# Experts' silu taken straight from its matmul bank, and the last two of eight holographic parts of six chunks computed wholly among the experts

## The chip, the core and the metric

The kernel runs on one core of a Trainium2 chip. The metric is the time of one execution in microseconds, as the device measures it; the median of some runs is compared. The engines are PE (matmuls), DVE (vectors), ACT (activations), POOL (vectors, without access to the matmul banks) and SP, which here issues DMAs.

## The reference, cut

Sixteen sequences of 256 tokens of width 128 go through two layers, each with a modulated layernorm before its attention part and its feed-forward part. The parts that the change touches are the first layer's mixture of experts and the second layer's attention, which is holographic (running sums of rotated values).

```
gu   = einsum('th,ehf->tef', x, gate_up_proj) + gate_up_bias      # 16 experts
gate = minimum(gu[..., ::2], 7.0);  up = clip(gu[..., 1::2], -7.0, 7.0)
glu  = gate * sigmoid(gate * 1.702)
out  = einsum('te,teh->th', scores, einsum('tei,eih->teh', (up + 1) * glu, down_proj) + down_bias)

k = exp(1j * 10 * (x @ Wk));  v = x @ Wv                          # 16 heads of 64: 1024 channels
out_pos   = real(cumsum(v * rotors) * conj(rotors)) / sqrt(t)
out_assoc = real(cumsum(v * conj(shifted k)) * k) / sqrt(t)
out = (out_pos * gate_0 + out_assoc * gate_1) @ Wo
```

The feed-forward part of the second layer that follows (`r * (square(relu(k)) @ W_v)`, called the mixing here) is not changed, only placed differently.

## The kernel before

The tokens lie in eight chunks of two sequences, 512 tokens each. Three stages follow one another. In each, every engine's instructions run in the order in which the program issues them, so an instruction that waits holds up all behind it on its engine.

**Attention** (to 301 us) covers all 16 sequences in 64 rounds; the change adds two operations on POOL there, at round 40.

**Experts** (301 to 687 us). One loop runs over n, 128 steps of chunk c and expert e (16 a chunk). In step n PE computes `pg` (gate, L808) and `pup` (up, L810) of expert n and `acc` (down, L833) of expert n-3. DVE forms `g` = min(pg + bias, limit) (L812); ACT forms `u` = pup + bias (L814) and the silu of g, back into the bank of pg (L817); POOL clips u (L818). One step later DVE multiplies, `u` = (u + 1) * pg (L824), and POOL weighs the product with the scores, `u` = u * wide (L825), which `acc` reads. Three banks serve pg, two pup, one acc.

Beside this, the same loop carries other work, each piece issued at a step of its own, all of it through one bank, `p_m`:

- at steps 3 and 4 of a chunk the last chunk's result is turned (`pmo`, L849) and added to the stream (DVE, L855), at steps 5 to 7 its means, squares and spread follow (ACT, POOL), and at step 7 the scores of the next chunk are transposed (`psc`, L339) and copied by ACT (`scT`), from which a DMA spreads them (`wide`);
- `parts_ahead` computes parts of the second layer's attention for six of the eight chunks. There are eight parts of 128 channels (j = 0 to 7) to a chunk. From step 8 of one chunk it normalizes the tokens of the chunk before (step 8), turns them (10), computes the values `pv` of part 7 (12) and its keys `pk` (13), and their phases: ACT rounds (`off`), DVE subtracts (`off`, L985, step 14), ACT takes |off|, and two Sin (steps 14 and 15). Then, in the next chunk, come pieces, one a step at 12 of the 16 steps: POOL binds a value row to a rotation (`bound_ahead`, L957), and at the step after DVE sums it along the tokens (L961), multiplies with gate and rotation (L965) and adds (L967). The pieces are four of part 7 by keys ("assoc"), four of part 7 by position ("pos"), and four of part 6 by position, whose values are computed at step 5. A DMA writes the two sums to memory (`there`).

**Holographic stage** (687 to 1052 us). One loop over steps, one for each part that is left: 7 for each of the first six chunks (`PARTS`), 8 for the last two. In a full step n POOL multiplies the sums of step n-1 with their phasors (L1456) and binds the values of step n+1 in two products (L1235); DVE runs two sums along the tokens (L1238), the phases of step n+2 (L1213) and one product (L1450); PE computes the keys and values of step n+3 (L1197, L1201) and adds the two products to `pout` (L1252, four matmuls). The seventh step of the first six chunks is a half one (`is_half`): part 6 by keys alone, since its position half was computed ahead. The sums computed ahead are fetched by DMA at a chunk's second step and added by one matmul each, at the fourth step and at the half step. `place` puts the mixing of earlier chunks into these steps, by their distance from the chunk's end; its tiles and the turned results (`pho`) share two banks, `p_x`.

Of the kernel before, what the change touches and what calls it, by code (L numbers as in the profile page):

```python
# [18 lines left out]
P = 128  # L19
# [16 lines left out]
ALPHA, LIMIT = 1.702, 7.0  # L36
GONE = -3.0e38
# [6 lines left out]
PARTS = [NJ - 1 if c < AHEAD else NJ for c in range(NCH)]  # L44
# [11 lines left out]
def tile_adaln_two_layers(ctx: ExitStack, tc: tile.TileContext, a: dict, out: bass.AP):  # L56
# [206 lines left out]
    with ExitStack() as moe_scope:  # L263
# [87 lines left out]
        with ExitStack() as scope:  # L351
# [374 lines left out]
            for n in range(len(rounds) + LAG + 1):  # L726
                if n < len(rounds):
                    if n in next_chunks:
                        start(project(next_chunks[n]), rank=0)
                    if n in (len(rounds) - NR, len(rounds) - NR + 1):  # L730
                        start(first_scores(n - (len(rounds) - NR)))
                    s = scores(n)
                    with_maxima(n, row_maxima(n, s))
                take_step("dve")
                if LAG <= n < len(rounds) + LAG:
                    es[n - LAG] = weights(n - LAG)
                if n >= LAG + 2 and rounds[n - LAG - 2][1] == NR - 1:
                    b = rounds[n - LAG - 2][0]
                    start(chunk_end(b // 2) if b % 2 else attn_end(b))
                if n > LAG:  # L740
                    values(n - LAG - 1, es.pop(n - LAG - 1))
                take_step("mid")
                take_step("end")
                take_step("take", True)
                if later_loads:
                    later_loads.pop(0)()
                if n == len(rounds) - 1:

                    for q in range(2):
                        widened(q)  # L750
                if n < LAG:

                    for place in ("mid", "end", "take"):
                        take_step(place)
                take_step("after", True)
                take_step("late")
                if n == 1:
                    filled(1, nc.gpsimd)
                    later_constants()
            take_step("take", True)  # L760
# [26 lines left out]
        with ExitStack() as scope:  # L787
# [16 lines left out]
            def gate_up(n, between=None):  # L804
# [6 lines left out]
                g = mp3.tile([P, N], F32, tag="g", name=f"g_{n}")  # L811
                nc.vector.tensor_scalar(g, pg, b_gu[:, 0, e : e + 1], LIMIT, ALU.add, ALU.min)  # L812
# [4 lines left out]
                nc.scalar.activation(pg, g, AF.Silu, scale=ALPHA)  # L817
                nc.gpsimd.tensor_scalar(u, u, LIMIT, -LIMIT, ALU.min, ALU.max)  # L818
                work[n] = pg, u

            def act(n):
                c, e = divmod(n, NE)
                pg, u = work.pop(n)
                nc.vector.scalar_tensor_tensor(u, u, 1.0, pg, ALU.add, ALU.mult)  # L824
                nc.gpsimd.tensor_tensor(u, u, wide[n // SOME][:, n % SOME, :], ALU.mult)  # L825
                work[n] = u
# [102 lines left out]
            def parts_ahead(c):  # L929
# [30 lines left out]
                def read(q, nm, k, s, i, probe):  # L960
# [11 lines left out]
                assoc = [(j, "assoc", k, s, 1, cs[:, s, k, 0:T], cs[:, s, k, 1:]) for k in range(2) for s in range(2)]  # L972
                pos_, pos_before = (
                    [(q, "pos", k, s, 0, rotor[:, q, s, :], rotor[:, q, s, :]) for k in range(2) for s in range(2)]
                    for q in (j, j - 1)
                )
                yield
                pk = p_m.tile([P, 2, T], F32, tag="m", name=f"pk0_{c}")
                nc.tensor.matmul(pk, w_k1[:, ts(j, P)], flat, start=True, stop=True)
                off, size = (  # L980
                    cross.tile([P, 2, T], F32, tag="hn4", name=f"{nm}_ahead_{c}") for nm in ("off", "size")
                )
                nc.scalar.activation(off, pk, AF.Copy, bias=ROUND)
                yield
                nc.vector.scalar_tensor_tensor(off, off, ROUND, pk, ALU.subtract, ALU.subtract)  # L985
                nc.scalar.activation(size, off, AF.Abs)
                nc.scalar.activation(cs[:, 1, :, 1:], off, AF.Sin, scale=-TWO_PI_IN)
                yield
                nc.scalar.activation(cs[:, 0, :, 1:], size, AF.Sin, bias=half_pi, scale=-TWO_PI_IN)
                yield  # L990

                pieces = assoc + pos_ + pos_before
                late_one = None
                for step in range(1, NE + 1):
# [6 lines left out]

                    if step not in (4, 7, 11, NE):
                        late_one = pieces.pop(0)
                        bind(*late_one[:4], late_one[5])
# [162 lines left out]
    with ExitStack() as scope:  # L1167
# [55 lines left out]
        def is_half(n):  # L1223

            return steps[n][0] < AHEAD and steps[n][1] == NJ - 2

# [3 lines left out]
        def binders(n):  # L1230
            w = work[n]
            v2 = w["v"].unsqueeze(1).to_broadcast(both)
            for nm, bind in (("pos", rot(n)), ("assoc", phasor[n % 3][:, :, :, 0:T]))[is_half(n) :]:
                w[nm] = hp.tile(both, F32, tag=f"bound_{nm}", name=f"bound_{nm}_{n}")
                nc.gpsimd.tensor_tensor(w[nm], v2, bind, ALU.mult)  # L1235

        def summed(n, nm, dst, half=slice(0, 2)):
            nc.vector.tensor_tensor_scan(  # L1238
                dst[:, half].rearrange("p s k t -> p (s k t)"),
                keep.rearrange("p (s k) t -> p s k t", k=2)[:, half].rearrange("p s k t -> p (s k t)"),  # L1240
                work[n][nm][:, half].rearrange("p s k t -> p (s k t)"),
# [176 lines left out]
        for n in range(last + 2):  # L1418
# [3 lines left out]
            place = {n - begin[m + 1]: m for m in (c - 2, c - 1) if 0 <= m < NCH - 1 and n <= last}  # L1422
# [5 lines left out]
            if j == 4 and AHEAD <= c + 1 < NCH:  # L1428
                into_tokens(c + 1, pt_tokens)
            if n <= last:  # L1430
                half = is_half(n)
                mem = p_mem.tile(both, F32, tag="mem", name=f"mem_{n}")
                if not half:
                    m_pos = hp.tile(both, F32, tag="m_pos", name=f"m_pos_{n}")
                m_assoc = hp.tile(both, F32, tag="sum_assoc", name=f"sum_assoc_{n}", bufs=3)
                work[n]["m"] = m_assoc
                if half:

                    summed(n, "assoc", mem, slice(0, 1))
                    summed(n, "assoc", m_assoc, slice(1, 2))  # L1440
                elif n:
                    summed(n, "assoc", m_assoc)
                if not half:
                    summed(n, "pos", mem)
                if n and n + 2 <= last:
                    phases(n + 2)
                if half:
                    nc.vector.tensor_tensor(m_assoc[:, 0], mem[:, 0], phasor[n % 3][:, 0, :, 1:], ALU.mult)
                else:
                    nc.vector.tensor_tensor(m_pos, mem, rot(n), ALU.mult)  # L1450
                if n == 0:
                    summed(n, "assoc", m_assoc)
            if 1 <= n <= last + 1:
                m = work.pop(n - 1)["m"]
                part = slice(1 if is_half(n - 1) else 0, 2)
                nc.gpsimd.tensor_tensor(m[:, part], m[:, part], phasor[(n - 1) % 3][:, part, :, 1:], ALU.mult)  # L1456
# [42 lines left out]
            if n < last:  # L1499
                if is_half(n):  # L1500
                    with_fetched(c, j, w_last[:, 0])
                else:
                    out_project(n, 0, w_pos, m_pos)
                if j == 1 and c < AHEAD:
                    fetched(c)
                if j == 3 and c < AHEAD:
                    with_fetched(c, NJ - 1, w_last[:, 1])
# [19 lines left out]
            if j == 1 and AHEAD <= c + 1 < NCH:  # L1527
                tokens(c + 1)
            if 2 in place:
                mix_means(place[2], hp, hp)  # L1530
            if j == 3 and AHEAD <= c + 1 < NCH:
# [127 lines left out]
```

## Time and profile before

| | |
|---|---|
| median of 3 runs | 1076.47 us (1075.56 to 1076.85) |
| the profiled execution: span from first to last instruction | 1073.6 us |
| the profiled execution: own time | not on the page; the median is 2.9 us above the span |
| busy: PE, DVE, ACT, POOL | 1020.8, 913.2, 705.0, 796.7 us |
| DMA moved | 53.15 MB |
| mean granted clock of PE | 0.994 |

Rows of a group name the line, the engine, the operation, what is written and read, the shapes and the count; then busy time and the mean of one in ns, and the idle time of the engine before them. A matmul of 512 columns appears as two records of 592 ns that start 430 ns apart, so that one is 0.86 us of PE; rows of one engine may overlap by some 50 ns.

### The profile page before, as it was taken

The page shows a single profiled execution, that of the slowest core. Times are in us where ns is not written, and L with a number is a line of the kernel's source. Part 1 is how long each engine was busy: PE and PEld are TensorE (multiplying, and loading weights), DVE is VectorE, ACT ScalarE, POOL GpSimd, SP SyncE. Part 2 cuts the span into 40 slices and gives each one's busy share as a digit, 9 for nine tenths or more (in the row PEclk, how much of TensorE's full clock was granted, in tenths as well). Part 3 has the DMA queues.
Part 4 walks back from the last instruction along what each step waited for, and adds up shares of the span by engine and source line. Part 5 has one row for each costly group of instructions (what it writes and reads, how often), then busy time and mean ns, then how long its engine had stood idle before and what let it go on. Part 6 is the DMA issues. An engine that isn't in the chain of part 4 may idle for free.

```text
span 1073.6 us, 16224 instructions
## 1 busy us (share of the span) xinstructions
PE 1020.8 (95%) x5333; PEld 518.4 (48%) x5333; DVE 913.2 (85%) x1413; ACT 705.0 (66%) x1515; POOL 796.7 (74%) x754
## 2 busy tenths in 40 slices
PE   7999999999999999999999999898999999999987
PEld 5566766676654444444434434333444444444334
DVE  6679878998756798988878778999999999999995
ACT  3776677667656677687766746355767767767662
POOL 3245334533557678888878788899999999999992
PEclk9999999999999999999999999999999999999999
DMA  4102100000052222323222223100000000000000
GB/s 118 42 11 71 51 5 3 2 4 2 4 179 96 82 99 79 118 91 107 100 98 89 89 89 108 59 10 10 14 7 30 15 15 30 1 11 5 5 10 20
DMA packets 35538, 53.15 MB, mean 50 GB/s; under 512 B 8416, under 2 KB 23296, under 8 KB 35456
## 3 DMA queue, kind: packets, MB, share of 16 engines
q1 hardware_dynamic: 34912, 51.87, 14.8%
q8 instruction: 42, 0.69, 0.2%
q14 instruction: 40, 0.33, 0.1%
q10 hardware_dynamic: 544, 0.26, 0.1%
HBM read 46.34 MB, written 5.51 MB: 48 GB/s over the span
## 4 chain that ended last, share of the span: by engine, by line
PE 64%; POOL 15%; DVE 10%; issue 5%; ACT 5%; DMA 1%; SPq 0%; DVEq 0%; POOLq 0%; ACTq 0%
PE pout L1252 9%; PE pg L808 7%; PE acc L833 7%; PE pup L810 7%; PE s L440 5%; PE st L474 5%; PE po L494 5%; POOL u L825 3%; POOL bound_assoc L1235 3%; POOL bound_pos L1235 3%; POOL sum_assoc L1456 2%; PE pk L1197 2%; PE pv L1201 2%; DVE sum_assoc L1238 2%; DVE mem L1238 2%
## 5 line engine op out<-in xcount | busy, mean ns | idle before, releaser
L482 ACT ACTIVATE exp<-st 128x512 f32<-128x512 f32 x256 | 132.2, 603 | 85.9 <-PE st L474 85.9
L452 DVE TENSOR_REDUCE maxima<-s 128x2 f32<-128x512 f32 x256 | 159.0, 685 | 25.7 <-PE s L440 25.3
L825 POOL TENSOR_TENSOR u<-u,wide 128x512 f32<-128x512 f32 x128 | 164.6, 1286 | 16.5 <-DVE u L824 7.4
L833 PE MATMUL acc<-u,w_dn 128*128 128x512 f32 x256 | 133.9, 605 | 6.1 <-POOL u L825 6.1
L1238 DVE TENSOR_TENSOR_SCAN sum_assoc<-keep,bound_assoc 128x1024 f32<-128x1024 bf16 (+1 forms) x58 | 126.0, 2173 | 9.9 <-POOL bound_assoc L1235 9.9
L808 PE MATMUL pg<-hT,w_gu 128*128 128x512 f32 x256 | 131.9, 597 | 0.8 <-DVE logits L674 0.4
L810 PE MATMUL pup<-hT,w_gu 128*128 128x512 f32 x256 | 130.7, 592 | 0.0
L814 ACT ACTIVATE u<-pup,b_gu 128x512 f32<-128x512 f32 x128 | 87.0, 679 | 63.7 <-PE pup L810 55.7
L1235 POOL TENSOR_TENSOR bound_assoc<-v,phasor 128x1024 f32<-128x1024 f32 x57 | 124.2, 2179 | 1.7 <-ACT phasor L1221 1.7
L818 POOL TENSOR_SCALAR u<-u 128x512 f32<-128x512 f32 x128 | 80.4, 628 | 59.6 <-ACT u L814 53.4
L812 DVE TENSOR_SCALAR g<-pg,b_gu 128x512 f32<-128x512 f32 x128 | 95.4, 746 | 32.7 <-PE pg L808 32.4
L1456 POOL TENSOR_TENSOR sum_assoc<-sum_assoc,phasor 128x1024 f32<-128x1024 f32 (+1 forms) x58 | 120.9, 2085 | 0.3 <-DVE sum_assoc L1238 0.3
L1238 DVE TENSOR_TENSOR_SCAN mem<-keep,bound_pos 128x1024 f32<-128x1024 bf16 x52 | 118.3, 2275 | 0.0
L1252 PE MATMUL pout<-m_pos,w_pos 128*128 128x512 f32 x204 | 98.4, 605 | 13.5 <-ACT oT L1277 10.7
L1235 POOL TENSOR_TENSOR bound_pos<-v,rotor 128x1024 f32<-128x1024 f32 x51 | 111.1, 2178 | 0.0
L1252 PE MATMUL pout<-sum_assoc,w_assoc 128*128 128x512 f32 x228 | 108.2, 597 | 1.5 <-POOL sum_assoc L1456 1.4
L817 ACT ACTIVATE pg<-g 128x512 f32<-128x512 f32 x128 | 76.3, 596 | 42.3 <-DVE g L812 41.9
L824 DVE SCALAR_TENSOR_TENSOR u<-u,pg 128x512 f32<-128x512 f32 x128 | 86.9, 679 | 11.8 <-POOL u L818 9.9
L474 PE MATMUL st<-qx,kx 32*128 32x256 f32 x1024 | 81.6, 387 | 1.2 <-DMA qx<-turned 1.1
L833 PEld LDWEIGHTS acc<-u,w_dn 128*128 128x128 f32 x256 | 46.7, 191 | 74.3 <-issue 42.9
L440 PE MATMUL s<-kx,qx 32*128 32x256 f32 x1024 | 78.0, 407 | 4.2 <-DVE kx L577 1.8
L1219 ACT ACTIVATE phasor<-off 128x512 f32<-128x512 f32 x56 | 35.1, 627 | 70.0 <-DVE off L1213 68.5
(301 smaller groups left out, 1912.2 us busy)
## 6 DMA issues: line engine op xcount, KB each, us to landing
wide<-scores SPq DMA_DIRECT2D x64, 512.0 KB
qx<-turned SPq DMA_DIRECT2D x256, 1.0 KB
there<-total SPq DMA_DIRECT2D x12, 256.0 KB
fetched<-there SPq DMA_DIRECT2D x12, 256.0 KB
w_gu<-in_gate_up_dram SPq DMA_DIRECT2D x8, 256.0 KB
out_dram<-x SPq DMA_DIRECT2D x16, 128.0 KB
x<-in_x_dram SPq DMA_DIRECT2D x14, 128.0 KB
w_dn<-in_down_dram SPq DMA_DIRECT2D x4, 256.0 KB
```

Of the source, the lines that this page charges most:

```text
L440: nc.tensor.matmul(s[g][:, i, :], qs[c][r][rows_, k, ts(i, P)], ks[c][rows_, r // NS, k, :], start=True, stop=True,)
L452: nc.vector.tensor_reduce(mx[:, :, g], s[g], AX.X, ALU.max, negate=True)
L474: nc.tensor.matmul(st[g][:, i, :], ks[c][rows_, r // NS, k, ts(i, P)], qs[c][r][rows_, k, :], start=True, stop=True,)
L482: nc.scalar.activation(e[:, g, :, :], st[g], AF.Exp, scale=QSCALE)
L808: nc.tensor.matmul(pg, w_gu[:, e, 0 : 2 * D : 2], h2, start=True, stop=True)
L810: nc.tensor.matmul(pu, w_gu[:, e, 1 : 2 * D : 2], h2, start=True, stop=True)
L825: nc.gpsimd.tensor_tensor(u, u, wide[n // SOME][:, n % SOME, :], ALU.mult)
L833: nc.tensor.matmul(accs[c], w_dn[:, e, :], work.pop(n), start=False, stop=(e == NE - 1))
L1235: nc.gpsimd.tensor_tensor(w[nm], v2, bind, ALU.mult)
L1238: nc.vector.tensor_tensor_scan(dst[:, half].rearrange("p s k t -> p (s k t)"), keep.rearrange("p (s k) t -> p s k t", k=2)[:, half].rearra ...
L1252: nc.tensor.matmul(pos[c], w[:, j, :], m[:, k, :, :].rearrange("p k t -> p (k t)"), start=(j == 0 and i == 0 and k == 0), stop=(c < NCH - ...
L1456: nc.gpsimd.tensor_tensor(m[:, part], m[:, part], phasor[(n - 1) % 3][:, part, :, 1:], ALU.mult)
```

## The change

It has two parts.

In the experts, `g` and its DVE instruction go. ACT takes the silu from the bank of pg with the bias in the activation, `silu(1.702 * pg + 1.702 * bias)`, ahead of `u`; the limit is taken after the silu, as the silu's value at the limit (`MOST`), in DVE's product. The +1 of `up + 1` goes into the bias and into POOL's bounds. Two operations on POOL scale and shift the biases once, in the attention stage.

In `parts_ahead`, part 6 is computed whole, with keys of its own: `pk` of part 6 at step 6 of the chunk, its `off` and |off| at step 7, its Sin at step 8. There are 16 pieces, one at every step. The holographic stage then has six full steps for each of the first six chunks and no half step; the fetched sums are added at the fourth and the fifth step, and the mixing spreads over up to three later chunks.

```diff
+MOST = ALPHA * LIMIT / (1.0 + math.exp(-ALPHA * LIMIT))
-PARTS = [NJ - 1 if c < AHEAD else NJ for c in range(NCH)]
+PARTS = [NJ - 2 if c < AHEAD else NJ for c in range(NCH)]
...
+                if n == 40:
+
+                    nc.gpsimd.tensor_scalar(b_gu[:, 0, :], b_gu[:, 0, :], ALPHA, None, ALU.mult)
+                    nc.gpsimd.tensor_scalar(b_gu[:, 1, :], b_gu[:, 1, :], 1.0, None, ALU.add)
...
-                g = mp3.tile([P, N], F32, tag="g", name=f"g_{n}")
-                nc.vector.tensor_scalar(g, pg, b_gu[:, 0, e : e + 1], LIMIT, ALU.add, ALU.min)
+                nc.scalar.activation(pg, pg, AF.Silu, bias=b_gu[:, 0, e : e + 1], scale=ALPHA)
                 u = mp3.tile([P, N], F32, tag="u", name=f"u_{n}", bufs=4)
                 nc.scalar.activation(u, pu, AF.Identity, bias=b_gu[:, 1, e : e + 1])
...
-                nc.scalar.activation(pg, g, AF.Silu, scale=ALPHA)
-                nc.gpsimd.tensor_scalar(u, u, LIMIT, -LIMIT, ALU.min, ALU.max)
+                nc.gpsimd.tensor_scalar(u, u, LIMIT + 1.0, 1.0 - LIMIT, ALU.min, ALU.max)
...
-                nc.vector.scalar_tensor_tensor(u, u, 1.0, pg, ALU.add, ALU.mult)
+                nc.vector.scalar_tensor_tensor(u, pg, MOST, u, ALU.min, ALU.mult)
...
+                def phasors(q):
+                    pk = p_m.tile([P, 2, T], F32, tag="m", name=f"pk0_{c}_{q}")
+                    nc.tensor.matmul(pk, w_k1[:, ts(q, P)], flat, start=True, stop=True)
...
+                    nc.scalar.activation(off, pk, AF.Copy, bias=ROUND)
+                    yield
+                    nc.vector.scalar_tensor_tensor(off, off, ROUND, pk, ALU.subtract, ALU.subtract)
+                    nc.scalar.activation(size, off, AF.Abs)
+                    yield
+                    nc.scalar.activation(cs[:, 1, :, 1:], off, AF.Sin, scale=-TWO_PI_IN)
+                    nc.scalar.activation(cs[:, 0, :, 1:], size, AF.Sin, bias=half_pi, scale=-TWO_PI_IN)
...
+                pieces = [*pieces_of(j), *pieces_of(j - 1)]
+                late_one, next_ones = None, None
+                for step in range(1, NE + 2):
                     yield
                     if late_one:
                         read(*late_one[:5], late_one[6])
                         late_one = None
                     if step == 5:
                         vs[j - 1] = values(j - 1)
-
-                    if step not in (4, 7, 11, NE):
+                    if step == 6:
+                        next_ones = phasors(j - 1)
+                    if next_ones:
+                        next_ones = next_ones if next(next_ones, 0) is None else None
+                    if pieces:
                         late_one = pieces.pop(0)
                         bind(*late_one[:4], late_one[5])
...
-            place = {n - begin[m + 1]: m for m in (c - 2, c - 1) if 0 <= m < NCH - 1 and n <= last}
+            place = {n - begin[m + 1]: m for m in (c - 3, c - 2, c - 1) if 0 <= m < NCH - 1 and n <= last}
...
-                if is_half(n):
-                    with_fetched(c, j, w_last[:, 0])
-                else:
-                    out_project(n, 0, w_pos, m_pos)
+                out_project(n, 0, w_pos, m_pos)
                 if j == 1 and c < AHEAD:
                     fetched(c)
-                if j == 3 and c < AHEAD:
-                    with_fetched(c, NJ - 1, w_last[:, 1])
+                if j in (3, 4) and c < AHEAD:
+                    with_fetched(c, NJ + 2 - j, w_last[:, 4 - j])
```

The rest of the diff takes `is_half` and its branches out, and counts the steps at which the last two chunks' tokens are prepared from a chunk's end.

## The prediction

> **What bounds the kernel now.** I read the page first, then the busy time by stretch, then each stage's groups and waits, and last the timeline around one step that the change fills. The kernel has three stages: attention (0 to 301 us), the experts (301 to 687 us) and the holographic stage (687 to 1052 us). The change leaves the first alone.
>
> ```profile
> PE 1020.8 (95%) x5333; PEld 518.4 (48%) x5333; DVE 913.2 (85%) x1413; ACT 705.0 (66%) x1515; POOL 796.7 (74%) x754
> core 0: us, PE busy (x) PEld busy (x) DVE busy (x) ACT busy (x) POOL busy (x), PEclk, DMA share, GB/s
> 488.10:534.50 46.40, 46.40 (x118) 20.91 (x117) 37.80 (x67) 36.33 (x87) 38.49 (x48) 1.00 0.29 103
> 783.90:827.20 43.30, 41.91 (x106) 18.86 (x106) 42.71 (x37) 30.72 (x67) 43.22 (x23) 1.00 0.06 19
> 827.20:870.60 43.40, 41.95 (x107) 18.97 (x107) 42.71 (x37) 30.94 (x67) 43.28 (x23) 1.00 0.06 19
> ```
>
> The first row is the whole kernel. The second gives the columns of the rest: 488.1 to 534.5 us is one chunk of the experts, the two others are one chunk each of the holographic stage. In the experts' chunk PE is busy for all 46.4 us and DVE, ACT and POOL have 8 to 10 us to spare. In a holographic chunk three engines are full at once: POOL 43.2, DVE 42.7, PE 41.9 of 43.3. So work taken out of the holographic stage is worth what it costs on the fullest of the three, and work put into the experts is worth what it costs PE, or makes PE wait. The clock is 1.00 in all of them.
>
> **What the holographic stage loses.** Six chunks have six full steps and one half step; the half step goes. These are its rows, all others are the full steps':
>
> ```profile
> L1235 POOL TENSOR_TENSOR bound_assoc<-v,phasor 128x1024 f32<-128x1024 f32 x57 | 124.2, 2179 | 1.7 <-ACT phasor L1221 1.7
> L1456 POOL TENSOR_TENSOR sum_assoc<-sum_assoc,phasor 128x512 f32<-128x512 f32 x6 | 7.6, 1267 | 0.0
> L1238 DVE TENSOR_TENSOR_SCAN mem<-keep,bound_assoc 128x512 f32<-128x512 bf16 x6 | 7.4, 1231 | 0.2
> L1238 DVE TENSOR_TENSOR_SCAN sum_assoc<-keep,bound_assoc 128x512 f32<-128x512 bf16 x6 | 7.2, 1204 | 0.0
> L1448 DVE TENSOR_TENSOR sum_assoc<-mem,phasor 128x512 f32<-128x512 f32 x6 | 4.2, 692 | 0.0
> L1213 DVE SCALAR_TENSOR_TENSOR off<-whole,pk 128x512 f32<-128x512 f32 x56 | 37.9, 676 | 0.0
> ```
>
> For each chunk POOL loses one bind (2.18 us, 2.13 from start to start) and a half product (1.27, 1.24 from start to start): 3.37 us. DVE loses 1.23 + 1.20 + 0.69 + 0.68 = 3.80. PE loses pk, pv and two pout; each is two records 0.43 us apart, so 4 x 0.86 = 3.44. The smallest counts, POOL's: 6 x 3.37 = 20.2 us. A chunk becomes 39.9 us. Nothing is late next by much, since the other two fall by more, but PE stays close: 41.9 - 3.4 = 38.5 busy, plus the one wait a chunk for oT (10.7 us over 7 times, 1.5 each), is 40.0. And the mixing that used seven steps is packed into six: in the changed kernel's order `pk2` falls in a chunk's second step and gets the bank of `pho`, which DVE gives back only at the end of its queue for that step. DVE runs ahead of PE there by up to a step, so I take no loss, and 1 us a chunk (6 in all) as the other end.
>
> **What the experts get.** PE gets one `pk` matmul more per chunk (the `pv` was there already): 6 x 0.86 = 5.1 us, on the path, since PE is full.
>
> DVE loses 128 g (0.746 us, 95.4 us in all) and gets 24 more pieces: 24 x (0.69 scan + 0.49 product) and 24 additions of 0.425, with 6 off of 0.68, 42.6 us. POOL gets 24 binds of 0.68, 16.4 us, and two 128x16 operations in the attention stage (a 128x4 one of the same kind takes 0.24), which nothing there waits for. ACT's silu takes its bias from a column now: 0.596 becomes about 0.69, because Sin with a bias column takes 0.712 and without one 0.614, 12 us in all; the other end is the 0.679 of `u`, which also reads PSUM. Six more phasors on ACT take 0.59 + 0.63 + 0.61 + 0.71 each, 15.3 us. All of this lies beside PE, which covers it: ACT has 10 us to spare in a chunk and needs 1.5 + 2.5. Without the cover it would cost 27 us.
>
> A rule speaks against putting more Sin between the silus: the Trainium skill, "ScalarE: Activation LUTs", section "What ACT_TABLE_LOAD costs", states about 2.66 us for each switch to another table set. Twelve more switches would by it be an estimated 32 us on ACT. The trace has 4 table loads (1.283 us each) in the whole execution, while the six groups of Sin at L987 and L989 already lie between silus with no load beside them. So the sum goes by the rows: no switch.
>
> What PE's waits in this stage are worth back:
>
> ```profile
> PE acc L833 <- POOL u L825: 6.1, 8, 1.6
> PE pk L979 <- ACT v_ahead L945: 1.7, 1, 1.7
> PE pv L1023 <- DVE x L855: 1.4, 1, 1.4
> PE pg L808 <- DVE logits L674: 0.4, 1, 0.4
> ```
>
> These are all of PE's waits there, with one more of 0.4. Where DVE falls behind, `u` comes late to POOL and so to PE. Two of the eight (1.3 and 1.6 us, at 682 and 685 us) are the last experts' own chain, which stays. Without g the rest of those should go: 6.1 - 2.9 + 1.4 + 0.8 = 5.4 us back; nothing at the other end.
>
> **The added wait.** `p_m` has one bank in this stage. In before, step 5 of a chunk puts pv into it and step 7 transposes the scores (`psc`) in it. The change puts a pk between them at step 6, whose last reader is DVE's `off`, issued at step 7 behind DVE's piece of that step, while `psc` is issued in step 7 on PE. Behind psc in PE's queue is the next expert. This is the stretch in before, of a chunk whose gate of step 7 starts at 508.64:
>
> ```profile
> start us, us, engine line op out<-in xcount [idle before <-releaser]
> 511.22 0.60 PE L339 MATMUL psc<-ident,scores 128*16 128x128 f32 x4
> 511.42 0.64 POOL L957 TENSOR_TENSOR und_ahead_pos<-v_ahead,rotor 128x256 f32<-128x256 f32 x1
> 512.10 0.70 DVE L961 TENSOR_TENSOR_SCAN sums<-sums,und_ahead_pos 128x256 f32<-128x256 f32 x1 [0.78 <-POOL und_ahead_pos L957]
> 512.83 0.49 DVE L965 SCALAR_TENSOR_TENSOR sums<-sums,gates,rotor 128x256 f32<-128x256 f32 x1
> 513.36 0.42 DVE L967 TENSOR_TENSOR total<-sums,total 128x256 f32<-128x256 f32 x1
> ```
>
> PE comes to psc at 511.22; with the pk ahead of it, at 512.08. DVE's piece of that step ends at 513.78, and it is not DVE's load that holds it but the bind on POOL (0.78 us of waiting), which in turn follows ACT's `u`; so the missing g does not bring it forward. With off (0.68) behind it the bank is free at 514.46. PE waits 2.4 us. The same distance shows at step 13, where pk is followed by an off in before: from pk to the end of off 5.4 to 8.3 us in the six chunks, and PE needs 3.4 of them for pk and three expert matmuls, which bounds the wait by 2.0 and 4.9; below nothing it cannot be. I take 2.4, by the rows at this very step. It happens where both pieces and scores are due, chunks 2 to 6: 5 x 2.4 = 12.0 us. ACT's copy of the scores and its |off| stand behind the same wait.
>
> Two small ones: pk at step 6 waits for ACT's copy of pv, which ends at 508.82 here where PE would come at 508.64, so about 0.2 a chunk, 1 us. And ACT in steps 5 to 8 has 4 silus and u (5.5), the means and squares (4.2), copies (1.7), phasor (1.9) and normed (1.9), 15.3 us against PE's 12.9; the two banks of pup and the three steps to `acc` hide some 3.5 us of lag, so I take 1 us in all, nothing and 15 as ends.
>
> **The sum.** The profiled execution has a span of 1073.6 us; its time outside the span is not on the page, and the median of the three runs, 1076.47, is 2.9 above it. -20.2 + 5.1 - 5.4 + 12.0 + 1 + 1 = -6.5: a span of 1067.1 and a time of 1070.0 us.
>
> **Rivals.**
>
> *The bank is free in time.* If DVE, rid of g, reaches off before PE reaches psc, the 12 us fall away: 1058. For it: DVE goes from 37.8 to about 33 of 46.4 us in a chunk. Against: the row above, where it waits for POOL.
>
> *ACT decides in steps 5 to 9: slower.* If silu with PSUM on both sides and a column costs more than 0.69, or ACT's in-order wait behind psc and off (2 us) comes on top of its 2.4 us of overload, the lag passes the 3.5 us that the banks hide. From there each microsecond of ACT is PE's. With 15 us of it (3 in each of five chunks), waits at 2.9 for psc and nothing back from DVE, the experts lose 5.1 + 14.5 + 1 + 15 = 35.6 against 20.2: 1092. It is slower than before by 0.2% from 22.4 us of loss on. Against: ACT idles 42 us for g in this stage, which goes.
>
> *The six-step chunks do not reach POOL's 39.9 us.* If PE, with oT's wait and pk2 behind pho, needs 41.2, then 6 x 2.1 = 12.6 us come back, not 20.2: 1077.6 with the rest as above, no change.
>
> **How the numbers follow.** 0.2% (2.15 us) is about what a measurement of this kernel can tell from no change. The forecast has 0.56, the free bank 0.2, ACT's overload 0.14, the unreached chunks 0.1. All of the second, nearly all of the first and part of the last are faster: 0.79; slower is the third and a little of the last, 0.16; between them 0.05. The range holds the forecast with its bounds (psc 2.0 to 4.9 a chunk, the return of 5.4 or none, 6 in the holographic stage) and reaches to the free bank on one side and past no change on the other: 1056 to 1079. The forecast's own range is 1063 to 1076.
>
> **What would show it.** Right: the holographic stage's pk and pv at 100 records each (112 now) and no 128x512 scans left; chunks of 39.6 to 40.2 us with POOL full; in the experts a wait of PE for DVE's off before psc, about 2.4 us five times; no wait of ACT for g. Wrong: no such wait; expert chunks longer than 50 us with PE waiting for POOL's u after step 8; a gap of PE before pk2 in each holographic chunk; more than 4 table loads.

## The result, and the profile after

The changed kernel takes 1088.5 us (median of four, 1083.6 to 1089.1) against 1076.66 before (four runs): a ratio of 1.0095, 95% interval 1.0076 to 1.0114. It is slower by 0.95%; the forecast was 1070.0 and faster. The profiled execution is the fastest of the four: 1083.62, span 1081.6. It is 8.0 us longer in span than the one before. The other three took 5 us more, at a mean granted clock of 0.986 to 0.989 against 0.993 (by their spans an estimated 4 to 7 us less of full clock); in which stretches it was lost, no profile shows.

The busy times of the whole, from the page:

```profile
PE 1010.5 (93%) x5297; PEld 512.0 (47%) x5297; DVE 854.2 (79%) x1339; ACT 712.3 (66%) x1509; POOL 791.9 (73%) x768
```

One chunk of the experts (chunk 4) and one of the holographic stage (chunk 3), busy time by stretch:

```profile
core 0: us, PE busy (x) PEld busy (x) DVE busy (x) ACT busy (x) POOL busy (x), PEclk, DMA share, GB/s
493.21:544.97 51.76, 48.30 (x119) 20.97 (x118) 35.40 (x65) 39.82 (x91) 41.71 (x53) 1.00 0.27 92
837.27:878.07 40.80, 38.47 (x99) 17.42 (x98) 39.30 (x33) 28.04 (x62) 39.66 (x22) 1.00 0.07 20
```

DVE has 59 us less to do, and the span grew. This chunk of the experts went from 46.4 to 51.8 us, and PE has holes in it where it had none. The holographic chunk went from 43.3 to 40.8, not to 39.9: POOL's 39.66 do not fill it.

Stages, from the starts of the first `pg`, of POOL's first product with a phasor and of its last (L1451; L1456 before):

| us | before | after | pk2_after | best7 |
|---|---|---|---|---|
| attention, to the first pg | 301.4 | 302.0 | 302.0 | 301.1 |
| experts, to the first product | 392.9 | 413.7 | 400.0 | 392.6 |
| holographic, first to last product | 354.8 | 341.7 | 333.2 | 333.1 |

So the experts lost 20.8 us and the holographic stage gave back 13.1 (the two other kernels are experiments, below). The waits of PE, and those of ACT and POOL that carry the story: engine and line, what it waited for, us in total, times, longest.

```profile
PE pout L1257 <- ACT oT L1282: 15.4, 7, 2.8
PE psc L340 <- DVE off_ahead L984: 10.6, 5, 2.7
PE acc L836 <- POOL u L828: 10.0, 12, 1.6
...
ACT size_ahead L985 <- DVE off_ahead L984: 24.1, 6, 6.4
...
POOL rstd_f L229 <- ACT off_f L222: 7.7, 5, 2.6
POOL phasor_ahead L974 <- DVE sums L968: 6.9, 5, 1.4
```

Two of them stood in before as well, and were shorter:

```profile
PE pout L1252 <- ACT oT L1277: 10.7, 7, 1.9
ACT size_ahead L986 <- DVE off_ahead L985: 10.6, 6, 3.6
```

`psc` is the wait that was forecast. This is the timeline of the stretch that was shown of before, step 7 of chunk 4:

```profile
518.55 0.73 POOL L960 TENSOR_TENSOR und_ahead_pos<-v_ahead,rotor 128x256 f32<-128x256 f32 x1
519.31 0.70 DVE L964 TENSOR_TENSOR_SCAN sums<-sums,und_ahead_pos 128x256 f32<-128x256 f32 x1 [1.14 <-POOL und_ahead_pos L960]
...
520.91 0.68 DVE L984 SCALAR_TENSOR_TENSOR off_ahead<-off_ahead,pk 128x512 f32<-128x512 f32 x1
521.65 0.60 PE L340 MATMUL psc<-ident,scores 128*16 128x128 f32 x4 [2.34 <-DVE off_ahead L984]
```

DVE waits for POOL's bind, reads the piece, then does `off`, and only then has PE the bank: 2.34 us, forecast 2.4.

What was not forecast stands at the chunk's turn. From start to start of `pg`, step 1 of chunks 3 to 7 took 4.13, 4.07, 4.13, 4.08 and 4.13 us, together 20.5; before, 15.0. The timeline between chunks 3 and 4, while PE goes from step 14 to step 1, is read from the top; the other engines run up to two steps behind PE.

```profile
489.81 0.11 POOL L974 MEMSET phasor_ahead<- 128x4 f32 x1 [1.38 <-DVE sums L968]
...
492.69 0.70 DVE L964 TENSOR_TENSOR_SCAN sums<-sums,und_ahead_pos 128x256 f32<-128x256 f32 x1 [1.35 <-POOL und_ahead_pos L960]
...
494.29 0.68 DVE L984 SCALAR_TENSOR_TENSOR off_ahead<-off_ahead,pk 128x512 f32<-128x512 f32 x1
...
495.00 0.63 ACT L985 ACTIVATE size_ahead<-off_ahead 128x512 f32<-128x512 f32 x1 [3.55 <-DVE off_ahead L984]
495.54 0.64 ACT L816 ACTIVATE pg<-pg,b_gu 128x512 f32<-128x512 f32 x1
496.11 0.68 ACT L818 ACTIVATE u<-pup,b_gu 128x512 f32<-128x512 f32 x1
496.87 0.61 POOL L821 TENSOR_SCALAR u<-u 128x512 f32<-128x512 f32 x1 [1.57 <-ACT u L818]
497.57 1.27 POOL L828 TENSOR_TENSOR u<-u,wide 128x512 f32<-128x512 f32 x1
498.89 1.13 PE L836 MATMUL acc<-u,w_dn 128*128 128x512 f32 x2 [0.92 <-POOL u L828]
```

At step 12 POOL's memset of the one phasor tile waits for DVE to read the old phasors; POOL's bind is late, DVE's read of it too, and `off` stands behind the read. ACT's |off| stands idle 3.55 us, and behind it in ACT's queue are the silu and `u` of step 15's expert. POOL's clip waits 1.57 us for that `u`, and behind the clip in POOL's queue stands the weighing of the expert before, which PE's down matmul waits for (0.92 us). Before, ACT's same wait was 10.6 us in all, and step 1 was shorter by the 5.6 us above.

### The profile page after: what moved, and what is told of

Same layout as the page of the kernel before. It is cut to its first block, busy times and chain, and to the rows that moved or that the text cites. A ratio compares the mean times of both kernels' runs of the same rounds, so it can differ in the third digit from the quotient of the medians.

```text
span 1081.6 us, 15970 instructions
## 1 busy us (share of the span) xinstructions
PE 1010.5 (93%) x5297; PEld 512.0 (47%) x5297; DVE 854.2 (79%) x1339; ACT 712.3 (66%) x1509; POOL 791.9 (73%) x768
## 4 chain that ended last, share of the span: by engine, by line
PE 51%; POOL 24%; DVE 12%; issue 7%; ACT 5%; DMA 1%; SPq 0%; DVEq 0%; POOLq 0%; ACTq 0%
PE pout L1257 9%; POOL u L828 9%; PE s L441 5%; PE st L475 5%; PE po L495 5%; DVE sums L964 4%; PE pup L815 3%; PE pg L813 3%; PE acc L836 3%; POOL bound_pos L1240 3%; POOL d_ahead_assoc L960 2%; POOL bound_assoc L1240 2%; PE pv L1210 2%; PE pk L1206 2%; POOL und_ahead_pos L960 2%
## 5 line engine op out<-in xcount | busy, mean ns | idle before, releaser
L827 DVE SCALAR_TENSOR_TENSOR u<-pg,u 128x512 f32<-128x512 f32 x128 | 87.6, 685 | 49.8 <-POOL u L821 49.7
L1243 DVE TENSOR_TENSOR_SCAN sum_assoc<-keep,bound_assoc 128x1024 f32<-128x1024 bf16 x52 | 118.6, 2281 | 10.1 <-POOL bound_assoc L1240 10.0
L816 ACT ACTIVATE pg<-pg,b_gu 128x512 f32<-128x512 f32 x128 | 83.9, 655 | 49.5 <-PE pg L813 49.1
L1257 PE MATMUL pout<-m_pos,w_pos 128*128 128x512 f32 x204 | 99.4, 610 | 18.2 <-ACT oT L1282 15.4
L1451 POOL TENSOR_TENSOR sum_assoc<-sum_assoc,phasor 128x1024 f32<-128x1024 f32 x52 | 113.7, 2186 | 0.3 <-DVE sum_assoc L1243 0.3
L1240 POOL TENSOR_TENSOR bound_assoc<-v,phasor 128x1024 f32<-128x1024 f32 x51 | 111.6, 2188 | 0.9 <-ACT phasor L1230 0.9
L1257 PE MATMUL pout<-sum_assoc,w_assoc 128*128 128x512 f32 x204 | 97.3, 599 | 3.0 <-POOL sum_assoc L1451 3.0
L836 PEld LDWEIGHTS acc<-u,w_dn 128*128 128x128 f32 x256 | 46.4, 191 | 80.3 <-POOL u L828 36.4
L815 PEld LDWEIGHTS pup<-hT,w_gu 128*128 128x128 f32 x256 | 50.1, 197 | 61.5 <-issue 50.1
L1228 ACT ACTIVATE phasor<-off 128x512 f32<-128x512 f32 x50 | 31.3, 626 | 63.1 <-DVE off L1222 62.5
```

What stands on the lines that cost most here:

```text
L815: nc.tensor.matmul(pu, w_gu[:, e, 1 : 2 * D : 2], h2, start=True, stop=True)
L836: nc.tensor.matmul(accs[c], w_dn[:, e, :], work.pop(n), start=False, stop=(e == NE - 1))
L1243: nc.vector.tensor_tensor_scan(dst.rearrange("p s k t -> p (s k t)"), keep.rearrange("p q t -> p (q t)"), work[n][nm].rearrange("p s k t - ...
L1257: nc.tensor.matmul(pos[c], w[:, j, :], m[:, k, :, :].rearrange("p k t -> p (k t)"), start=(j == 0 and i == 0 and k == 0), stop=(c < NCH - ...
L1451: nc.gpsimd.tensor_tensor(m, m, phasor[(n - 1) % 3][:, :, :, 1:], ALU.mult)
```

## Experiments: which part costs

All times are medians against the kernel before on the same chip (1076.0 to 1077.8 us); ratios with 95% intervals.

**silu_alone**: before with the silu part only. **parts_alone**: the changed kernel with the silu part taken back (its `g`, silu, limits and product as before).

> The kernel before with the first part of the change alone: silu reads the gate's bank with a bias column, the limit sits in DVE's product, no g; parts 6 and 7 are shared out as in before (half step kept). Theory (the added waits all belong to the moved part): DVE loses 0.746 us a step, PE's waits for u go, chunk 1 gains the 1.9 us that it gained in the changed kernel and the later chunks at least as much: 4 to 10 us faster than before, 1067 to 1072. Rival (the silu path itself delays u, which now stands behind silu on ACT, and makes the stalls of step 1): expert chunks 3 to 7 have a PE step 1 of about 4.1 us, and the time is 1077 to 1085.

> The changed kernel with the silu path of before (g on DVE, silu from g, limits as in before); part 6 wholly between the experts, six full steps a chunk. Theory (the two parts add): the changed kernel's 1088.5 plus what the silu path gives, 4 to 10: 1092 to 1099; waits for psc and the step 1 stalls at least as in the changed kernel. Rival (the silu path makes the step 1 stalls): no more step 1 stalls than in before, 1078 to 1086.

Measured: 1072.93 (0.9955, 0.9939 to 0.9972) and 1088.16 (1.0101, 1.0080 to 1.0121). silu_alone's median is 3.6 us below before's, just short of its theory (4 to 10); in its profile the experts take 387.9 us, 5.0 less than before. But beside the moved part the silu gives nothing: 1088.2 without it, 1088.5 with it. Neither theory of parts_alone foresaw that the parts do not add. Its steps show why: step 1 of chunks 3 to 7 takes 15.9 us in all, the wait before psc is 11.6, and other steps are late instead. So beside the moved part the silu costs 4.6 us at step 1, about the 5.0 that it saves alone; u_first, below, tests why.

## Experiments: the experts' stalls

**off_first**: off ahead of the read.

```diff
+                    if step == 6:
+                        next_ones = phasors(j - 1)
+                    if next_ones:
+                        next_ones = next_ones if next(next_ones, 0) is None else None
                     if late_one:
                         read(*late_one[:5], late_one[6])
...
-                for steps_ in ahead:
+                for steps_ in reversed(ahead) if e == 14 else ahead:
```

> The changed kernel with DVE's off issued ahead of the read of the same step, at steps 7 and 14; nothing else. Theory (off stands behind a read that waits for POOL's bind, and ACT's |off| and PE's psc wait for off): PE's wait before psc falls from 2.4 a chunk to under 0.6, the PE step 1 of chunks 3 to 7 from 4.1 to under 3.0 us, ACT's wait of 24 us before |off| to under 10; together 14 to 19 us: 1070 to 1075. Rival (it is the load of a piece at every step, or the memset's wait, that makes step 1 late): only the 11 us of psc come back, step 1 stays above 3.7, 1077 to 1079.

**cs_once**: `cs` allocated once ahead of `parts_ahead`, with its memset.

> The changed kernel with the phasor tile between the experts allocated and its first column zeroed once, so that POOL's memset of step 12 (which waits 6.9 us over 5 times for DVE's read) is gone; nothing else. Theory (off behind read makes the stalls): the memset's 1.4 us of POOL a chunk is recovered by step 14, at most 0.4 us a chunk of the time moves: 1085.5 to 1089. Rival (the memset's wait makes POOL late, and from there the step 1 stalls): step 1 falls from 4.1 to under 3.0 and the time by 6 to 8: 1080 to 1083.

**abs_later**: the `yield` between off and |off|.

```diff
                     nc.vector.scalar_tensor_tensor(off, off, ROUND, pk, ALU.subtract, ALU.subtract)
-                    nc.scalar.activation(size, off, AF.Abs)
                     yield
+                    nc.scalar.activation(size, off, AF.Abs)
```

> The changed kernel with ACT's |off| issued one step after DVE's off (steps 8 and 15, ahead of the two Sin) instead of in the same step; off still stands behind the read. Theory (the stall of step 1 is ACT's queue: silu and u of step 14 stand behind |off|, which waits for an off that is itself late): ACT's wait for off falls from 24 us to under 6, step 1 of chunks 3 to 7 from 4.1 to 2.6 to 3.0, PE's wait before psc stays at about 2 a chunk; 5 to 8 us less: 1080 to 1084. Rival (off holds DVE's own product back, ACT's wait is beside it): step 1 stays above 3.7, 1086 to 1090.

**u_first**: the silu's line behind that of `u`.

> The changed kernel with ACT's u issued ahead of its silu in each step, as before the change; nothing else. Theory (ACT's queue stands still behind |off|; with silu ahead of u the clip on POOL and the expert's down matmul get u 0.66 us later than with u first, which is why the silu path gave nothing together with the moved part): step 1 of chunks 3 to 7 falls from 4.1 to 3.0 to 3.5 as in parts_alone, 3 to 6 us less: 1082 to 1086. Rival (the order of the two is hidden, it is only the wait for off): step 1 stays at 4.1, 1087 to 1090.

| | us | ratio (95%) | step 1 of chunks 3 to 7, sum | PE waits for off before psc |
|---|---|---|---|---|
| changed kernel | 1088.5 | 1.0095 (1.0076 to 1.0114) | 20.5 | 10.6 |
| off_first | 1070.91 | 0.9931 (0.9912 to 0.9950) | 14.3 | 3.5 |
| cs_once | 1078.21 | 1.0019 (1.0004 to 1.0035) | 15.8 | 10.5 |
| abs_later | 1078.34 | 1.0012 (0.9999 to 1.0026) | 14.4 | 10.4 |
| u_first | 1081.03 | 1.0033 (1.0020 to 1.0045) | 17.4 | 9.9 |

Four edits at four links of one chain, and each shortens step 1. abs_later is the clean one: off stays where it is, as late as it was, and PE's wait before psc stays; only ACT comes to |off| a step later. Its wait there falls from 24.1 to 11.9 us (expected: under 6), and step 1 falls by 6.1 us. So the step 1 stall is ACT's queue. u_first leaves that queue as late and only lets `u` out of it 0.66 us sooner; step 1 falls by 3.1 us, and the time by 7.5, more than its theory's 3 to 6. cs_once shows that my theory was too narrow: the 6.9 us that the memset waits are on the chain as well, and without them ACT's wait falls from 24.1 to 16.6; the time fell below even the rival's range. (In its profiled execution, which took 1085.3, step 8 of three chunks is 1.2 to 1.7 us late, of one in the changed kernel; that is PE's clock, see the last section.) off_first repairs both stalls:

```profile
PE psc L340 <- DVE off_ahead L984: 3.5, 4, 1.1
...
ACT size_ahead L985 <- DVE off_ahead L984: 7.0, 5, 2.7
```

Step 1 is not all of it: by the medians abs_later and cs_once gained 10 us each, of which step 1 gave 6.1 and 4.7. The changed kernel's profiled execution lies 4.9 us below its median, so the rest stands in no profile.

With the order of two DVE instructions changed at two steps of a chunk, the change is worth 0.7% instead of costing 0.95%.

**pk_at_8**: part 6's pk two steps later, behind psc; this needs the phasors two steps later, another order of pieces and two phasor tiles.

```diff
-                    if step == 6:
+                    if step == 8:
                         next_ones = phasors(j - 1)
...
-                pieces = [*pieces_of(j), *pieces_of(j - 1)]
+                a, b = [*pieces_of(j)], [*pieces_of(j - 1)]
+                pieces = a + b[4:6] + b[0:4] + b[6:8]
```

> The changed kernel with part 6's pk at step 8 instead of 6, behind psc; the pieces in the order assoc 7, pos 7, two pos 6, assoc 6, two pos 6; two phasor tiles allocated and zeroed once, so no memset at step 12. Theory (psc waits because the bank is held by the pk ahead of it): the wait for off before psc is gone, steps 7 and 8 are 3.0 and 3.4, and from the 1078.2 without the memset 10 to 13 us fall: 1065 to 1068. Rival (the wait goes with the off: the next user of the bank, the transposes of step 10, or the binds behind the later phasors, wait instead): 1074 to 1080.

Measured: 1078.60 (1.0016, 1.0005 to 1.0027). The rival was right. The wait for off before psc is gone and stands two steps later, at the transposes of step 10, the bank's next user:

```profile
PE pln_a L249 <- DVE off_ahead L987: 7.0, 4, 2.0
```

And in chunk 5 step 8 took 9.2 us, because the pk met the first holographic step's own keys (`first_steps`), which use the same bank and keep out of other steps only; part of that step is the clock, which was at half for 6.8 us around the end of the 3.7 us wait there. Another place in the one bank does not help while off comes late. Whether a second bank would, was not tried.

## Experiments: the holographic stage

Chunks 0 and 1 take 39.67 us in the changed kernel, where 39.9 was forecast, but chunks 2 to 6 take 42.2, 40.8, 40.8, 41.3 and 55.1. They are the ones that carry the mixing from its place 6 on. Of chunk 2's 42.2 us 1.7 are the clock: it is 0.96 in that chunk, and u_first, whose holographic stage is the same, took 40.5 us at 1.00 (the changed kernel, then u_first, columns as above):

```profile
795.10:837.27 42.17, 39.40 (x97) 17.84 (x96) 39.03 (x31) 27.98 (x62) 39.71 (x22) 0.96 0.05 13
790.80:831.27 40.47, 37.70 (x97) 17.05 (x96) 38.88 (x31) 27.68 (x62) 39.66 (x21) 1.00 0.04 13
```

The excess stands where POOL waits for ACT's figures before `rstd` (7.7 us), so I took ACT for late, with the sigmoid and the figures in one step, and tried three times to relieve it on top of off_first.

**off_spread**: `mix_spread` behind `binders`. **off_figures4**: besides, `mix_figures` at place 4. **sigmoid_10**: `mix_sigmoid` at place 10, with what follows it a step later, rstd and figures as in the changed kernel.

> off_first with POOL's two mixing operations (rstd, less) of the holographic stage issued behind the two binds of their step instead of ahead of them; nothing else. Theory (POOL, the fullest engine, stands 7.7 us in five chunks at rstd for ACT's figures, because in a six-step chunk the sigmoid and the figures fall in one step): chunks 2 to 5 of the holographic stage go from 42.2, 40.8, 40.8 and 41.3 to 39.7 to 40.2, chunk 6 from 55.1 to 52.5, together 6 to 9 us: 1062 to 1065. Rival (ACT is late there whatever POOL does, since PE's keys and oT hold it: the wait turns up at bound_assoc or at PE's pk): 1069 to 1072.

> off_spread with ACT's figures of the mixing (four squares and their scale) at place 4 instead of 3, a step in which ACT has no other mixing work; nothing else. Theory (off_spread only moved the wait from rstd to bound_assoc: it is ACT that is late, as sigmoid and figures, 1.7 and 2.4 us, fall in one step of a six-step chunk): chunks 2 to 5 of the holographic stage go from 40.8 to 39.7, chunk 6 from 55.2 to 53 to 54; 4 to 7 us less than off_spread: 1061.5 to 1064.5. Rival (rstd comes too late for the norm a step later, ACT waits there instead): 1066 to 1071.

> off_first with the mixing's sigmoid on ACT one step later (place 10 instead of 9), and with it DVE's two gated products (11 and 12), PE's transposes (12) and the two additions (both at 13); figures stay at place 3, rstd ahead of the binds, as in the changed kernel. Theory (in six steps the sigmoid, 1.7 us of ACT, falls into the step of the figures and ahead of them, so off_f is late by that for POOL's rstd): POOL's wait for off_f goes, chunks 2 to 5 of the holographic stage take 39.7 to 40.0 us, chunk 6 52.3 to 53.5; 6 to 9 us less than off_first: 1062 to 1065. Rival (ACT is late in these steps whatever is put in them, because PE's keys and oT hold it): the chunks stay at 40.8 to 41.3, 1068.5 to 1071.5.

Measured: 1068.38 (0.9927, 0.9914 to 0.9940), 1066.83 (0.9899, 0.9883 to 0.9915), 1069.49 (0.9927, 0.9912 to 0.9943), against 1070.91. No theory held: off_figures4 and sigmoid_10 lie in their rivals' ranges, off_spread 0.6 us below its rival's. Chunk 4 took 40.81, 40.82 and 40.81 us; only chunk 2 (by 1.1 to 1.8 us) and chunk 6 (by 1.4 in off_figures4) came clearly down, and chunk 3 took 42.4 in off_figures4, with the clock at half for 3.4 us in it. POOL's wait goes and comes back ahead of another instruction, as in off_spread's waits:

```profile
POOL bound_assoc L1240 <- ACT phasor L1230: 7.3, 6, 2.6
```

A wait that moves and keeps its length points to another engine. The busy times of chunk 3 at the top tell whose: PE is busy for 38.47 us of the 40.80, and waits 2.33 for oT, which makes 40.80. This is the timeline of that wait in the changed kernel:

```profile
838.03 0.58 ACT L1207 ACTIVATE whole<-pk 128x512 f32<-128x512 f32 x1
838.87 0.59 ACT L1211 COPY v<-pv 128x512 f32<-128x512 f32 x1 [0.26 <-PE pv L1210]
839.35 1.03 ACT L255 ACTIVATE shifted<-pln_f,mod 128x256 f32<-128x256 f32 x2
840.26 0.85 ACT L1282 ACTIVATE oT<-pout,gaT 128x256 f32<-128x256 f32 x2
841.16 1.98 PE L1257 MATMUL pout<-m_pos,w_pos 128*128 128x512 f32 x4 [2.33 <-ACT oT L1282]
```

In a chunk's first step PE may start the new `pout` only when oT has left its one bank. oT stands in ACT's queue behind the copies of that step and, since the mixing spans six steps, behind `shifted` too (place 6, which before fell on the half step).

**oT_early**: oT ahead of the two copies, and so of `shifted`. **pk2_after**: besides, the mixing's `pk2` behind the keys and values of its step on PE.

```diff
+            if j == 0 and c:
+                o = gated_out(c - 1)
             if n + 3 <= last:
                 projected(n + 3)
+            if 7 in place and n < last:
+                mixed(place[7], wk_now, wk_before, "pk2")
```

(The first two added lines are oT_early, the last two pk2_after; each is taken out of its old place.)

> off_first with ACT's oT (the gated copy of a chunk's sum, which frees PE's one bank for it) issued ahead of the whole and v copies of that step instead of behind them; nothing else. Theory (PE is the bound of the middle chunks: 38.5 us of work and 2.3 of waiting for oT, 40.8; ACT and POOL are late because they follow PE): PE's wait for oT falls from 15 us to under 6, chunks 2 to 5 take 39.7 to 40.0 us, chunk 6 52.5 to 54; POOL's wait for rstd goes without any change to the mixing; 5 to 8 us less than off_first: 1063 to 1066. Rival (ACT is late for its own load): the wait for oT goes but the chunks stay at 40.5 to 41.3: 1068.5 to 1071.5.

> oT_early with PE's pk2 (the mixing's keys, in the bank that pho gives back) issued behind the keys and values of that step instead of ahead of them; nothing else. Theory (PE bounds the middle chunks by its waits; the last one is pk2 behind pho): the wait for DVE's x before pk2 goes, chunks 3 to 5 take 39.7 to 39.9 us; 1.5 to 3 us less than oT_early: 1062 to 1064. Rival (the 0.7 us left in a chunk are POOL's wait for ACT's figures, behind the sigmoid): chunks stay at 40.4, 1064.5 to 1067.

Measured: 1065.20 (0.9904, 0.9887 to 0.9920) and 1062.16 (0.9862, 0.9841 to 0.9883). With oT early the wait for oT falls from 15.4 to 2.6 us. Chunks 3 and 4 fall to 40.4, not to the 39.7 to 40.0 expected, and chunk 2 to 39.7, and a wait of PE shows that the wait for oT had hidden:

```profile
PE pk L1310 <- DVE x L1295: 5.8, 4, 1.5
```

This is pk2 behind pho's bank. With that gone as well, chunks 0 to 5 take 39.65 to 39.71 us and chunk 6 53.0, and POOL is the bound (pk2_after, chunk 3, busy time by stretch):

```profile
820.93:860.59 39.66, 38.78 (x99) 17.30 (x98) 39.01 (x33) 28.01 (x62) 39.58 (x21) 1.00 0.08 20
```

POOL's wait for the figures fell to 0.5 us, though nothing was done to ACT's mixing. The stage takes 333.2 us, 21.6 less than before.

## Experiments: the repairs together

Each kernel has off ahead of the read, the pk at step 8 with two phasor tiles, and, but for the first, `first_steps` kept out of steps 8 and 9. pk8_off_spread adds off_spread's edit; best1 the edits of off_figures4 and u_first, best2 the same without u_first; best5 has u_first and sigmoid_10's edit; best6 u_first and oT early; best7 pk2_after's edit besides.

> All repairs together: pk of part 6 at step 8 with two phasor tiles zeroed once, off ahead of the read of its step, rstd and less behind the binds. Theory (three separate waits, so their prices add): the 1070.9 of off_first less 4 to 5 (the rest of psc), 1 to 3 (memset) and 6 to 9 (rstd): 1054 to 1060. Rival (they share one cover, so that the second repair finds less): 1060 to 1066.

> All repairs: off ahead of its read, part 6's pk at step 8 with two phasor tiles, the first steps' keys and values kept out of steps 8 and 9 too (in pk8_off_spread one of them met part 6's pk and cost PE about 6 us in one step), rstd behind the binds with figures at place 4, and u ahead of silu on ACT. Theory: 1065.4 less 5 to 6 (that step), 4 to 7 (figures), 0 to 2 (u first): 1051 to 1057. Rival (the repairs share cover): 1057 to 1062.

> best1 with silu ahead of u on ACT, as in the changed kernel. Theory (with off and |off| in time ACT's queue never stands still, so the order of the two costs nothing): within 1.5 us of best1. Rival (u first always brings the clip and the down matmul forward): 2 to 5 us above best1.

> The experts' repairs of best1 (off ahead of its read, part 6's pk at step 8 with two phasor tiles, first steps kept out of steps 8 and 9, u ahead of silu) with the sigmoid at place 10 in place of the two changes of rstd and figures. Theory: best1's 1058.6 less 4 to 6: 1052.5 to 1055. Rival (ACT is late whatever is put there): 1058 to 1061.

> The experts' repairs of best1 (off ahead of its read, part 6's pk at step 8 with two phasor tiles, first steps kept out of steps 8 and 9, u ahead of silu) and oT early; rstd, figures and sigmoid where the changed kernel has them. Theory: 1052 to 1055. Rival: 1057 to 1061.

> best6 with pk2 behind the keys and values of its step. Theory: 1.5 to 3 us less than best6: 1055.5 to 1057.5. Rival: 1058 to 1060.

| | us | ratio (95%) |
|---|---|---|
| pk8_off_spread | 1065.43 | 0.9894 (0.9881 to 0.9907) |
| best1 | 1058.61 | 0.9826 (0.9807 to 0.9844) |
| best2 | 1058.95 | 0.9825 (0.9808 to 0.9842) |
| best5 | 1062.34 | 0.9855 (0.9837 to 0.9874) |
| best6 | 1058.78 | 0.9843 (0.9828 to 0.9857) |
| best7 | 1053.43 | 0.9776 (0.9760 to 0.9793) |

best1 against best2 answers the order of silu and `u`: 7.5 us in the changed kernel, nothing measurable here. Once ACT's queue no longer stands still, it does not matter what stands in it first. pk8_off_spread missed its theory: step 8 of chunk 5, which pk_at_8 had shown, took 8.7 us in it and 3.4 in best1, and off_spread's edit brought little. best1, best5 and best6 missed theirs by no more than what their holographic stage still lost (337.4, 341.8 and 337.5 us against best7's 333.1); best7 gained more than expected, since chunk 6 fell as well (54.7 to 53.0). best7 is 2.2% faster than before and beats both kernels; its experts take 392.6 us with part 6 whole, as long as before without it.

## Why the prediction was wrong, step by step

- **The holographic stage, 20.2 us: the failed step.** 13.1 arrived: chunks 0 and 1 gave 3.4 us each, chunks 2 to 5 0.9, 2.3, 2.6 and 2.5, and chunk 6, which loses no part, took 1.8 longer (55.1 against 53.3). I had the right numbers in hand: PE's 38.5 busy (38.47 in the window), plus the wait for oT. I took that wait at the 1.5 us of before; it became 2.3 in the middle chunks (15.4 us over seven times; 10.7 before), since the mixing that moved into six steps put an ACT instruction ahead of oT. And my 40.0 for PE already stood above POOL's 39.9, which I passed over. pk2 behind pho, taken at nothing with 1 us a chunk as the other end, was 1.5 in four chunks once oT was early. The rival "the six-step chunks do not reach POOL's 39.9" had the mechanism, and I gave it one chance in ten. That its 12.6 us lie so near the 13.1 is partly luck: it had neither the two chunks that do reach 39.7, nor chunk 6, nor the 1.7 us of clock in chunk 2.
- **ACT's lag, 1 us: the other failed step.** The ends were nothing and 15; step 1 alone grew by 5.6. I looked at steps 5 to 9, where operations are added. It came at steps 12 to 17, where the waits of before grew. At step 14 off stood behind a read in before too; new there is a memset that has a reader to wait for, and without that wait (cs_once) step 1 is 4.7 us shorter. What else made off later is not taken apart. The rival "ACT decides", which ended slower, had engine and sign. Its "in-order wait behind psc and off" came at step 7 (9.5 us in five waits for psc) and, unforeseen, behind off at step 14 (24.1 us), and abs_later shows that step 1 is late by the second.
- **The wait before psc, 12.0 us: right.** By PE's steps 7 of chunks 2 to 6, 4.81, 5.88, 5.52, 4.81 and 5.42 against 3.01, it cost 11.4. The cause was read rightly too (POOL's bind holds DVE, and the missing g does not help), but not the next thought: off needed no place behind that read.
- **pk, 5.1 us: right.** Step 6 went from 2.58 to 3.43 in six chunks. The wait of pk for the copy of pv, 1 us, did not come: 3.43 is the step without a wait.
- **The return of 5.4: right in size where it is alone** (5.0 in silu_alone's experts), partly by luck. Of the waits it was made of, that of pk for the copy of pv (1.7), 0.8 of pv's for x and the two for POOL's `u` in chunk 1 (1.4) went. But new waits for `u` came in later chunks, and their sum is 6.1 us in silu_alone as in before. In the changed kernel that sum is 10.0, and the return is lost.
- **Silu at 0.69 us**: 0.655 (128 times). **Table loads**: the Trainium skill, "ScalarE: Activation LUTs", section "What ACT_TABLE_LOAD costs", would have charged each switch of tables; the profile has the 4 loads of before, 1.283 us each, with twelve more Sin among the silus.
- **The sum**: the experts' 20.8 are 5.1 + 11.4 + 5.6 and, net, 1.3 less elsewhere (with 1.7 of clock at step 8 of chunk 6 in it), against 13.7 in the forecast's sum. These 7.1 and the 7.1 that the holographic stage kept back are 14.2 of the 14.5 us between the forecast's span of 1067.1 and 1081.6.

## What to carry to other kernels

Where engines run in order, do not price a new or longer wait by the instruction that waits: list what stands behind it in its queue, and ask whether the waiting instruction could be issued a step later, or what it waits for a step earlier; here moving one of them was worth 10 to 18 us by the medians. When a stage loses work on its fullest engine, add up the next engine with its waits, and price those anew in the new order, not by the old trace. If an edit moves a wait from one instruction to the next and the stage keeps its length, the bound is another engine.

## What the runs showed of the hardware that was not expected

- A wait of PE may cost more than its length. In the changed kernel's profile the granted clock is 0.50 from 628.9 to 632.3 us, right after a wait of 2.24 for off before psc, and 0.51 from 799.5 to 802.9, after a wait of 2.77 for oT; step 8 of chunk 6 is 1.7 us longer there, and so is chunk 2 above. In all kept profiles every such stretch that begins between 305 and 1000 us, 3.4 or 6.8 us long, begins inside a wait of PE of 1.5 us or more or less than 2 us after one. The reverse does not hold: of the five waits before psc in the changed kernel one was followed by half clock, of the same five in cs_once three, which are its three late steps 8. What decides it is not shown.
- The same program's runs can lie far apart: those of the changed kernel 5.5 us and those of cs_once 7.8, but those of silu_alone 0.6 and of best7 0.7. How much of this the clock makes is not shown either: cs_once's runs at 0.986 took 1077.5 and 1078.0 us, its run at 0.994 took 1077.7.
- The attention stage, in which all these kernels differ by two small operations at most, took 301.1 us (best7) to 305.5 us (cs_once) in the profiled executions: 4 us that belong to no edit (the clock was at half for 3.4 and for 6.8 us at its start, an estimated 1.7 of them), so that a stage has to be compared with the same stage, not spans with spans.
- The gap that repeats in each chunk before `pout` is what the Trainium skill, "Perfetto Trace Analysis", section "Optimization Strategy", calls a consistent bubble, which it says can mean too little memory for the next tile. The trace agrees that the one bank of pout was waited for seven times, 15.4 us; but no second bank was needed to shorten it: issuing its reader ahead of the two copies and `shifted` left 2.6 us in oT_early, and 5.0 in pk2_after, where the chunks reach POOL's 39.7.
